# Two attention blocks in fp32 on one core: layer 1's value product as a two-level product, its row sums on VectorE and its differences on GpSimd, with other ends

## The chip, the cores and the metric

The kernel runs on one core of a Trainium2 chip. A time is the time in microseconds of one execution of the whole program on the device. Three executions of the kernel before took 2806.8, 2808.33 and 2808.77 us; their median, 2808.33 us, stands for it. A further execution was taken with the hardware profiler: that is where all shorter times in this text come from. TensorE is called PE in the profile, VectorE DVE, ScalarE ACT, GpSimd POOL, and SyncE, which issues nearly all the transfers, SP.

## The reference

The input is a batch of 8 images with 512 channels and 32 x 32 = 1024 positions. Two attention blocks follow one another, each with its own weights. In short:

```python
def block0(x):                                # 32 groups, 8 heads of 64 channels
    h = group_norm(x, gn_weight, gn_bias)     # per image and group
    q, k, v = split_by_head(w_qkv @ h + b_qkv)
    weight = softmax((q * scale)^T @ (k * scale))   # 1024 x 1024 per head
    a = weight @ v
    return x + w_proj @ a + b_proj

def block1(x):                                # 8 groups, one head of 512 channels
    h = group_norm(x, gamma, beta)
    q, k, v = (conv1x1(h, w, b) for w, b in ((q_w, q_b), (k_w, k_b), (v_w, v_b)))
    o = softmax((q^T @ k) * 512 ** -0.5) @ v
    return x + conv1x1(o, p_w, p_b)

out = block1(block0(x))
```

All of it is in float32.

## The kernel before

**Products in halves.** Every product of two large matrices is done by the Strassen-Winograd scheme: both factors are cut in two by two, seven products of quarters take the place of eight, and sums of quarters are formed before and after. `wino` (L229) does this on one level: products 1, the four of `middle`, 4 and 3, in this order, the last two put off into the list `tail`, so that the next product's first matmuls come between. `conv2` (L508) does it on two levels, 49 products in all, with the steps of `inner_steps` (L439). There, results are added up in SBUF by VectorE (`add`, L526, and L537 in the groups) and by GpSimd (`more`, L539 and L542). The sums of an image's quarters that two levels need, the dictionary `inner`, are formed once by `inner_factors` (L410) on GpSimd; those of a weight are formed in the prologue (`prepare`, `keep` and `keep2`), stored in DRAM (`wdram` one level, `wdram2` two), and loaded for each use by `load_weight` in the order of the list `uses`, through three buffers. A two-level weight takes two loads (1792 and 1344 KB), a one-level weight one (1792 KB).

**Layer 1's matrices are folded.** Queries and keys become one matrix m, so the scores are h^T m h, with g = m h; the value and the output convolution become one matrix z. Per image layer 1 has four products: g (`layer1_scores`, two levels), the scores (`scores1`, one level outside and one inside), z (L1093, `by_token`, one level: 56 matmuls of 256 columns) and the weighted sum (`values1`, one level). In layer 0 the convolutions v, k, q and p are two-level products, and the attention goes head by head.

**The order.** The loop over b interleaves the layers: layer 0's attention of image b, then layer 1 of image b-1 (g, scores, z, weighted sum), then v, k and q of image b+1 and the projection of image b. The first image's v, q and k, and the weights' preparation, are in `prologue`, and the first attention (b = 0) still carries a part of that preparation, in the lists `later` that name the attention step at which each is issued. Image 7 goes without partner, so the last layer 1 stands alone at the end. Each engine works off its own queue in program order. Where an operation of VectorE or GpSimd isn't tied to a place by `keep_in_program_order`, a scheduler sets it among its neighbours. Small work is handed over as lists: `hooks` (run after a product), and `background`, from which `run_background` takes a few after each product.

**Around the change.** In `scores1` seven outer products s = 0..6 stand for p = 1, 2, 5, 6, 7, 3, 4. In each, PSUM tiles are added into the eight tiles `e` by VectorE (L729), and in s = 3 and s = 4 also among themselves by GpSimd (`more`, L734). `exps` (L737) turns a quarter into exponentials on ScalarE once it is complete. `add_up` (L741) then adds the eight quarters' halves into `total`, the rows' sums over the keys (up to the partition sum, which TensorE does in `sums`): on GpSimd, L743. Last, `right_sums` (L163, used at L786) forms four differences of exponentials, t1, t2, t4 and b22 - b12, for the weighted sum: the two 128x1024 tiles of the first two on VectorE and of the last two on GpSimd. In `values1`, `done` (L797) turns a finished quarter of the output into x + (product * 1/sum) + bias with three VectorE operations (L802, L803, L805) and stores it.

Of the kernel before, what the change touches and what calls it, by code (L numbers as in the profile page):

```python
# [29 lines left out]
def two_attention_blocks_kernel(  # L30
# [143 lines left out]
    def main_path(ctx):  # L174
# [54 lines left out]
        def wino(uid, mm, done, middle=(6, 2, 5, 7), hooks=(), after=(), back=2):  # L229
# [12 lines left out]
            def step(p):  # L242
                n = bank[p]
                for i in range(2):
# [11 lines left out]
                    elif p == 7:  # L256
                        upper(u3, i, "w")
                        done(i, 1, 1, ps["c", i], u3[i])
                    elif p == 4:
                        done(i, 1, 0, ps["b", i], t1[i])  # L260
                    elif p == 3:
                        done(i, 0, 1, ps["c", i], u2[i])
# [31 lines left out]
        def keep(n, t):  # L294
            nc.sync.dma_start(wdram[n], t)


        wdram2 = {n: dram.tile([P, 7, 7, P], F32, name=f"sums2_{n}") for n in "qkmvp"}

        def keep2(n, t, engine=nc.gpsimd):  # L300
# [9 lines left out]
            for dst, x, y, op in (  # L310
                (s1, a21, a22, ALU.add), (s2, s1, a11, ALU.subtract), (s3, a11, a21, ALU.subtract),
                (s4, a12, s2, ALU.subtract),
            ):
                tc.keep_in_program_order(engine.tensor_tensor(dst, x, y, op))
            for j, f in enumerate((a11, a12, s4, a22, s1, s2, s3)):
                nc.sync.dma_start(wdram2[n][:, :, j, :], f)
# [4 lines left out]
        for b in range(1, B - 1):  # L321
            uses += [*twice["m"], "z", *layer0, *twice["p"]]
        uses += ["p", *twice["m"], "z"]
        uses += [*twice["m"], "z"]
# [385 lines left out]
        def scores1(f, gf, gsteps, first, uid, stats):  # L710
# [8 lines left out]
            parts = [pair_tile(f"sum{r}_{uid}") for r in range(2)]  # L719
# [21 lines left out]
            def add_up(r, c):  # L741

                on = lambda dst, x, y: lambda: tc.keep_in_program_order(nc.gpsimd.tensor_tensor(dst, x, y, ALU.add))  # L743
                if r == c:
                    return [on(parts[r], e[c, 0, r], e[c, 1, r])]
                return [
                    *(on(parts[r], parts[r], e[c, cc, r]) for cc in range(2)),
                    on(total[:, r, :], parts[r][:, 0, :], parts[r][:, 1, :]),
                ]

            def product(s, p, y, x, before, small, after7=(), final=()):
# [21 lines left out]
            product(3, 6, (1, 0), (1, 0), [7, 3], [])  # L773
            product(4, 7, (1, 0), (1, 0), [], stats[5:7])
            product(5, 3, (0, 1), (0, 1), [], stats[7:10] + add_up(0, 0), [lambda: exps(1, 1)], [lambda: exps(0, 1)])
            product(
                6, 4, (1, 0), (1, 0), [], stats[10:] + add_up(1, 1) + add_up(0, 1), (),
                [lambda: exps(1, 0), lambda: background.extend(add_up(1, 0) + steps)],
            )

            t = [[pair_tile(f"t{n}_{uid}_{cc}") for cc in range(2)] for n in (1, 2, 4)]
            engines = [nc.vector] * 4 + [nc.gpsimd] * 4
            fs, steps = right_sums(
                [(e[0, cc, 0], e[0, cc, 1]) for cc in range(2)], [(e[1, cc, 0], e[1, cc, 1]) for cc in range(2)],
                [lambda cc, n=n: t[n][cc] for n in range(3)],
                lambda *a: engines.pop(0).tensor_tensor(*a, ALU.subtract),  # L786
            )
            return total, {p: [x[:, i, :] for x in fs[p] for i in range(2)] for p in fs}

        def values1(b, zf, ef, r, xt, uid, hooks):  # L790
            def mm(p, i, ps, start):
                for k in range(4):
                    matmul(
                        ps, zf[p][k // 2][:, k % 2, ts(i, P)], ef[p][k], start=start and k == 0, stop=k == 3, skip_group_check=True
                    )
# [607 lines left out]
```

## Time and profile before

| | us |
|---|---|
| median of three executions | 2808.33 |
| the profiled execution | 2808.09 |
| its span, from the first to the last instruction | 2806.3 |
| TensorE busy | 2786.6 |
| VectorE busy | 1981.4 |
| GpSimd busy | 1265.5 |
| ScalarE busy | 986.3 |
| the first attention (119.38 to 242.33) | 122.95 |
| the second attention (331.70 to 447.56) | 115.86 |
| TensorE's clock, granted share over the span | 0.998 |

Busy time is the time in which an instruction of the engine ran; the span less the busy time is idle. Matmuls overlap one another, so the duration of one matmul in the list of groups is longer than its share of the time; the distance from one start to the next is its cost. A line of a group gives the line of the code, the engine, the operation, output and inputs with the shapes, how many there were, their busy time and mean duration in ns, and the idle time ahead of them with the instruction that ended it. A line of the timeline gives start and duration in us first, for several instructions of one kind in a row (x2) as one. An fp32 matmul leaves two records in the trace.

### The profile page before, as it was taken

Reading aid. Unit: us, or ns where it says so; the run is one execution under the profiler, and the core shown is the slowest. Engines: PE = TensorE matmul, PEld = TensorE weight load, DVE = VectorE, ACT = ScalarE, POOL = GpSimd, SP = SyncE. Lnnn points to the kernel's source line nnn. Section 1 sums busy time; section 2 is a strip of 40 time slices with the busy share of each in tenths; the row PEclk is TensorE's granted clock in tenths of the full one; section 3 lists DMA queues with packets and bytes.
Section 4 is the critical chain, followed back from the end, with each engine's and each line's share of the span. In section 5 each row is a group of like instructions: output and inputs, shape, how many; then the busy total and the mean of one; then the engine's idle time right before and its main releaser. Section 6 shows DMA issues by size and latency. Waiting matters only on the chain.

```text
span 2806.3 us, 35081 instructions
## 1 busy us (share of the span) xinstructions
PE 2786.6 (99%) x12756; PEld 1749.4 (62%) x12756; DVE 1981.4 (71%) x3018; ACT 986.3 (35%) x1275; POOL 1265.5 (45%) x1300
## 2 busy tenths in 40 slices
PE   9999999999999999999999999999999999999999
PEld 5436736776376853768538594485844868348584
DVE  5477777667776777766776767766678756787665
ACT  1253354214632146312463125531255212633130
POOL 2302705745067440774308652185521846137572
PEclk9999999999999999999999999999999999999999
DMA  8744512234123441134401343114521035112301
GB/s 285 226 161 139 196 32 70 111 146 178 34 67 131 152 153 39 62 139 165 148 24 62 150 174 127 32 54 161 187 102 49 37 151 207 63 55 94 120 5 73
DMA packets 118525, 320.10 MB, mean 114 GB/s; under 512 B 19591, under 2 KB 57927, under 8 KB 107722
## 3 DMA queue, kind: packets, MB, share of 16 engines
q1 hardware_dynamic: 117758, 317.36, 31.7%
q8 instruction: 103, 1.69, 0.2%
q14 instruction: 76, 0.62, 0.1%
q10 hardware_dynamic: 588, 0.42, 0.0%
HBM read 247.13 MB, written 70.62 MB: 113 GB/s over the span
## 4 chain that ended last, share of the span: by engine, by line
PE 97%; DVE 2%; issue 1%; POOL 1%; DMA 0%; ACT 0%; SPq 0%; DVEq 0%; POOLq 0%
PE sc L60 16%; PE av L60 15%; PE psb_av L60 6%; PE psb L60 5%; PE psa_av L60 4%; PE psc_av L60 4%; PE psc L60 3%; PE psa L60 3%; PE psb_z L60 3%; PE psb_g L60 3%; PE psb_k L60 3%; PE psb_q L60 3%; PE psb_v L60 3%; PE psb_p L60 2%; PE psa_z L60 2%; PE psc_z L60 2%
## 5 line engine op out<-in xcount | busy, mean ns | idle before, releaser
L658 ACT ACTIVATE e<-sc 128x1024 f32<-128x1024 f32 x512 | 476.2, 1051 | 79.7 <-PE sc L60 79.7
L662 DVE TENSOR_TENSOR sum<-sum,e 128x1024 f32<-128x1024 f32 x384 | 470.5, 1225 | 35.8 <-ACT x L138 0.5
L60 PE MATMUL sc<-q,k 64*128 64x512 f32 x2048 | 458.4, 597 | 0.0
L60 PE MATMUL av<-e,v 128*64 128x512 f32 x2048 | 453.4, 595 | 0.0
L60 PEld LDWEIGHTS sc<-q,k 64*128 64x128 f32 x2048 | 190.7, 186 | 247.3 <-ACT e L658 120.3
L60 PEld LDWEIGHTS av<-e,v 128*64 128x64 f32 x2048 | 141.4, 137 | 299.0 <-issue 289.0
L421 POOL TENSOR_TENSOR inner_h<-x 128x256 f32<-128x256 f32 x16 | 14.8, 924 | 415.8 <-DVE x L1105 415.8
L660 DVE TENSOR_TENSOR sum<-e,e 128x1024 f32<-128x1024 f32 x64 | 79.2, 1237 | 103.7 <-ACT e L658 103.7
L681 ACT COPY a<-av 128x512 f32<-128x512 f32 x64 | 37.6, 587 | 319.4 <-PE av L60 308.1
L126 POOL TENSOR_TENSOR rstd<-ve,mhalf 128x4 f32<-128x4 f32 x16 | 16.7, 1043 | 263.9 <-DVE ve L124 263.9
L60 PE MATMUL psb<-inner,inner_h 128*128 128x256 f32 x448 | 115.6, 380 | 0.0
L60 PE MATMUL psa_av<-e,z 128*128 128x512 f32 x256 | 113.3, 595 | 0.0
L421 POOL TENSOR_TENSOR inner_h<-h 128x256 f32<-128x256 f32 x30 | 24.1, 805 | 186.9 <-DVE h L1105 119.8
L743 POOL TENSOR_TENSOR sum<-sum,e 128x1024 f32<-128x1024 f32 x32 | 81.4, 2543 | 28.9 <-ACT e L739 27.7
L60 PEld LDWEIGHTS psb<-inner,inner_h 128*128 128x128 f32 x448 | 84.5, 190 | 13.6 <-POOL inner L436 1.8
L469 ACT COPY psb_v<-psa_v 128x512 f32<-128x512 f32 (+1 forms) x28 | 14.5, 517 | 218.9 <-DVE x L805 155.1
L60 PE MATMUL psb_g<-inner_h,w_m 128*128 128x256 f32 x336 | 86.5, 385 | 0.3
L729 DVE TENSOR_TENSOR e<-psc,u 128x512 f32<-128x512 f32 x56 | 38.7, 691 | 65.5 <-PE psc L60 65.3
L542 POOL TENSOR_TENSOR v<-v,v 128x256 f32<-128x256 f32 x28 | 20.1, 727 | 143.5 <-DVE u_v L537 143.4
L60 PEld LDWEIGHTS psa_av<-e,z 128*128 128x128 f32 x256 | 48.0, 190 | 57.3 <-issue 56.6
L421 POOL TENSOR_TENSOR inner_h<-t_h 128x256 f32<-128x256 f32 x62 | 73.3, 1187 | 21.3 <-PE psc_av L60 16.1
L739 ACT ACTIVATE e<-e 128x1024 f32<-128x1024 f32 x64 | 65.3, 1053 | 46.7 <-DVE e L729 25.6
(433 smaller groups left out, 6088.6 us busy)
## 6 DMA issues: line engine op xcount, KB each, us to landing
r<-all_rows SPq DMA_DIRECT2D x78, 256.0 KB
x<-in_x SPq DMA_DIRECT2D x36, 512.0 KB
h<-in_x SPq DMA_DIRECT2D x32, 512.0 KB
spill<-x SPq DMA_DIRECT2D x32, 512.0 KB
x<-spill SPq DMA_DIRECT2D x32, 512.0 KB
out<-x SPq DMA_DIRECT2D x64, 256.0 KB
kept<-a SPq DMA_DIRECT2D x28, 512.0 KB
again<-kept SPq DMA_DIRECT2D x28, 512.0 KB
```

Source lines behind the costliest of these rows:

```text
L60: tc.keep_in_program_order(nc.tensor.matmul(*args, **kw))
L126: nc.gpsimd.tensor_tensor(rstd, ve, mhalf, ALU.pow)
L421: pin(engine.tensor_tensor(dst, x, y, ALU.subtract))
L469: nc.scalar.copy(ps["b"], ps["a"])
L542: nc.gpsimd.tensor_tensor(d, x, y, ALU.add)
L658: nc.scalar.activation(e, sc, AF.Exp, scale=(C // 8) ** -0.5)
L660: nc.vector.tensor_add(total, es[0], e)
L662: nc.vector.tensor_add(total, total, e)
L681: nc.scalar.copy(dst, av)
L729: nc.vector.tensor_add(dst[0], ps, x[0])
L739: nc.scalar.activation(e[c, cc, r], e[c, cc, r], AF.Exp, scale=scale)
L743: on = lambda dst, x, y: lambda: tc.keep_in_program_order(nc.gpsimd.tensor_tensor(dst, x, y, ALU.add))
```

## The change

Layer 1's z becomes a two-level product: `layer1_rest` calls `conv2` by tokens with the image's `inner`, which is kept until then. Its weight is prepared twice over in the first attention (`keep2_steps`, four GpSimd operations of 128x896 and seven stores of 448 KB each), and loaded in two parts per image. The result's layout is another, so `mm` in `values1` and `halves` index it differently.

In `scores1` the row sums move from GpSimd (six additions of 128x1024 and two of 128x512 per image) to VectorE: fourteen additions of 128x512 per image straight into `total`; three are handed over in product s = 3, three in s = 6, and eight after it, so that they fall into z's first products. The tiles `parts` are gone. The differences are now eight GpSimd operations in the order b12' = b22 - b12 (two), t2 = b12' + b11, t1 = b22 - t2, t4 = b21 - t2; the first two are handed over after z's second pair of products, the other six after its fourth.

In the last image `early` adds bias and x to the half-finished quarter ahead of the last product, and that product is cut in two column halves for its last tile, so that one multiplication, one addition and one store of half a tile remain per half. In the prologue `normed` is called one matmul earlier, and the preparation of k moves behind v. In the first attention z's preparation steps move from step 1 to step 3, and weight loads from steps 2, 2, 5 to steps 4, 12, 12. The layer 1 of image 6 gets the last image's group mean and affine steps two products earlier.

```diff
@@ -226,7 +226,7 @@
-        def wino(uid, mm, done, middle=(6, 2, 5, 7), hooks=(), after=(), back=2):
+        def wino(uid, mm, done, middle=(6, 2, 5, 7), hooks=(), after=(), back=2, early=None):
@@ -257,6 +257,8 @@
                     elif p == 4:
+                        if early:
+                            early(i, u2[i])
                         done(i, 1, 0, ps["b", i], t1[i])
@@ -292,12 +294,12 @@
         def keep(n, t):
-            nc.sync.dma_start(wdram[n], t)
-
-
-        wdram2 = {n: dram.tile([P, 7, 7, P], F32, name=f"sums2_{n}") for n in "qkmvp"}
-
-        def keep2(n, t, engine=nc.gpsimd):
+            return nc.sync.dma_start(wdram[n], t)
+
+
+        wdram2 = {n: dram.tile([P, 7, 7, P], F32, name=f"sums2_{n}") for n in "qkmvpz"}
+
+        def keep2_steps(n, t, engine=nc.gpsimd):
@@ -307,21 +309,32 @@
             s1, s2, s3, s4 = u
-            for dst, x, y, op in (
-                (s1, a21, a22, ALU.add), (s2, s1, a11, ALU.subtract), (s3, a11, a21, ALU.subtract),
-                (s4, a12, s2, ALU.subtract),
-            ):
-                tc.keep_in_program_order(engine.tensor_tensor(dst, x, y, op))
-            for j, f in enumerate((a11, a12, s4, a22, s1, s2, s3)):
-                nc.sync.dma_start(wdram2[n][:, :, j, :], f)
+            def store():
+                for j, f in enumerate((a11, a12, s4, a22, s1, s2, s3)):
+                    tc.keep_in_program_order(nc.sync.dma_start(wdram2[n][:, :, j, :], f))
+
+            return [
+                *(
+                    lambda dst=dst, x=x, y=y, op=op: tc.keep_in_program_order(engine.tensor_tensor(dst, x, y, op))
+                    for dst, x, y, op in (
+                        (s1, a21, a22, ALU.add), (s2, s1, a11, ALU.subtract), (s3, a11, a21, ALU.subtract),
+                        (s4, a12, s2, ALU.subtract),
+                    )
+                ),
+                store,
+            ]
+
+        def keep2(n, t, engine=nc.gpsimd):
+            for f in keep2_steps(n, t, engine):
+                f()
         twice = {n: [(n, 0), (n, 1)] for n in wdram2}
         layer0 = [*twice["v"], *twice["k"], *twice["q"]]
         uses = [*layer0, *twice["p"]]
         for b in range(1, B - 1):
-            uses += [*twice["m"], "z", *layer0, *twice["p"]]
-        uses += ["p", *twice["m"], "z"]
-        uses += [*twice["m"], "z"]
+            uses += [*twice["m"], *twice["z"], *layer0, *twice["p"]]
+        uses += ["p", *twice["m"], *twice["z"]]
+        uses += [*twice["m"], *twice["z"]]
         loaded = []
@@ -716,7 +729,6 @@
             total = pair_tile(f"sum_{uid}")
-            parts = [pair_tile(f"sum{r}_{uid}") for r in range(2)]
             g2 = {1: first}
@@ -740,13 +752,11 @@
-                on = lambda dst, x, y: lambda: tc.keep_in_program_order(nc.gpsimd.tensor_tensor(dst, x, y, ALU.add))
+                on = lambda *a: lambda: tc.keep_in_program_order(nc.vector.tensor_add(*a))
+                dst, terms = total[:, r, :], [e[c, cc, r][:, i, :] for cc in range(2) for i in range(2)]
                 if r == c:
-                    return [on(parts[r], e[c, 0, r], e[c, 1, r])]
-                return [
-                    *(on(parts[r], parts[r], e[c, cc, r]) for cc in range(2)),
-                    on(total[:, r, :], parts[r][:, 0, :], parts[r][:, 1, :]),
-                ]
+                    return [on(dst, *terms[:2]), *(on(dst, dst, t) for t in terms[2:])]
+                return [on(dst, dst, t) for t in terms]
@@ -770,42 +780,69 @@
             product(2, 5, (1, 1), None, [6, 4], gsteps[4:] + stats[3:5])
-            product(3, 6, (1, 0), (1, 0), [7, 3], [])
+            product(3, 6, (1, 0), (1, 0), [7, 3], add_up(0, 0))
             product(4, 7, (1, 0), (1, 0), [], stats[5:7])
-            product(5, 3, (0, 1), (0, 1), [], stats[7:10] + add_up(0, 0), [lambda: exps(1, 1)], [lambda: exps(0, 1)])
+            product(5, 3, (0, 1), (0, 1), [], stats[7:10], [lambda: exps(1, 1)], [lambda: exps(0, 1)])
             product(
-                6, 4, (1, 0), (1, 0), [], stats[10:] + add_up(1, 1) + add_up(0, 1), (),
-                [lambda: exps(1, 0), lambda: background.extend(add_up(1, 0) + steps)],
+                6, 4, (1, 0), (1, 0), [], stats[10:] + add_up(1, 1), (),
+                [lambda: exps(1, 0), lambda: background.extend(add_up(0, 1) + add_up(1, 0))],
             )
-            t = [[pair_tile(f"t{n}_{uid}_{cc}") for cc in range(2)] for n in (1, 2, 4)]
-            engines = [nc.vector] * 4 + [nc.gpsimd] * 4
-            fs, steps = right_sums(
-                [(e[0, cc, 0], e[0, cc, 1]) for cc in range(2)], [(e[1, cc, 0], e[1, cc, 1]) for cc in range(2)],
-                [lambda cc, n=n: t[n][cc] for n in range(3)],
-                lambda *a: engines.pop(0).tensor_tensor(*a, ALU.subtract),
-            )
-            return total, {p: [x[:, i, :] for x in fs[p] for i in range(2)] for p in fs}
+            t1, t2, t4 = ([pair_tile(f"t{n}_{uid}_{cc}") for cc in range(2)] for n in (1, 2, 4))
+            b11, b12, b21, b22 = ([e[c, cc, r] for cc in range(2)] for c in range(2) for r in range(2))
+            on = lambda *a: lambda: tc.keep_in_program_order(nc.gpsimd.tensor_tensor(*a))
+            steps = [
+                on(dst[cc], x[cc], y[cc], op) for dst, x, y, op in (
+                    (b12, b22, b12, ALU.subtract), (t2, b12, b11, ALU.add), (t1, b22, t2, ALU.subtract),
+                    (t4, b21, t2, ALU.subtract),
+                ) for cc in range(2)
+            ]
+            fs = {1: b11, 2: b21, 3: b22, 4: t4, 5: t1, 6: t2, 7: b12}
+            return total, {p: [x[:, i, :] for x in fs[p] for i in range(2)] for p in fs}, steps
+
         def values1(b, zf, ef, r, xt, uid, hooks):
+            last = b == B - 1
+
             def mm(p, i, ps, start):
-                for k in range(4):
-                    matmul(
-                        ps, zf[p][k // 2][:, k % 2, ts(i, P)], ef[p][k], start=start and k == 0, stop=k == 3, skip_group_check=True
-                    )
+                cut = 2 if last and (p, i) == (3, 1) else 1
+                for part in range(cut):
+                    cols = ts(part, HT // cut)
+                    for k in range(4):
+                        matmul(
+                            ps[:, cols], zf[p][i][:, ts(k, P)], ef[p][k][:, cols],
+                            start=start and k == 0, stop=k == 3, skip_group_check=True,
+                        )
+
+            def added(xh, o, oc):
+                nc.vector.scalar_tensor_tensor(xh, o, obias[1][:, oc : oc + 1], xh, ALU.add, ALU.add)
+
+            def early(i, u):
+                xh = xt[i][:, ts(1, HT)]
+                nc.vector.tensor_mul(u, u, r[:, 1, :])
+                added(xh, u, i)
             def done(i, row, c, ps, u):
                 oc = 2 * row + i
+                xh = xt[oc][:, ts(c, HT)]
+                dst = out[b, oc * P : (oc + 1) * P, ts(c, HT)]
+                if last and (row, c) == (0, 1):
+                    cut = 2 if i == 1 else 1
+                    for part in range(cut):
+                        cols = ts(part, HT // cut)
+                        nc.vector.tensor_mul(ps[:, cols], ps[:, cols], r[:, c, cols])
+                        nc.vector.tensor_add(xh[:, cols], ps[:, cols], xh[:, cols])
+                        nc.sync.dma_start(dst[:, cols], xh[:, cols])
+                    return
                 o = acc_tile(f"o_{uid}_{oc}_{c}") if (row, c) == (1, 1) else ps
                 if u is not None:
                     nc.vector.tensor_add(o, ps, u)
                 nc.vector.tensor_mul(o, o, r[:, c, :])
-                xh = xt[oc][:, ts(c, HT)]
-                nc.vector.scalar_tensor_tensor(xh, o, obias[1][:, oc : oc + 1], xh, ALU.add, ALU.add)
-                nc.sync.dma_start(out[b, oc * P : (oc + 1) * P, ts(c, HT)], xh)
-
-            wino(f"av_{uid}", mm, done, middle=(2, 5, 6, 7), hooks=hooks, back=4)
+                added(xh, o, oc)
+                nc.sync.dma_start(dst, xh)
+
+            wino(f"av_{uid}", mm, done, middle=(2, 5, 6, 7), hooks=hooks, back=4, early=early if last else None)
@@ -888,19 +925,19 @@
             product(
-                wq, wk, "m", {6: lambda: norm.group_mean(acc_tile("gmean_0_0")[:, :KC]), 9: normed},
+                wq, wk, "m", {6: lambda: norm.group_mean(acc_tile("gmean_0_0")[:, :KC]), 8: normed},
             )
             raw_v = raw("v", 6)
             raw_p = raw("p", 7)
             for f in first["v"][1]:
                 f()
             background.extend(steps)
-            for n in "qk":
-                background.extend(first[n][1])
+            background.extend(first["q"][1])
             v = by_token(weight_factors(first["v"][0]), hf, "v0_0", middle=(2, 5, 6, 7), back=4)
             finish()
             run_background(len(background))
             keep2("v", first["v"][0], nc.vector)
+            background.extend(first["k"][1])
             x1 = [load_x(1, c, "x1") for c in range(KC)] if B > 1 else []
@@ -924,9 +961,10 @@
             load = lambda: load_weight(tc.keep_in_program_order)
+            second = keep2_steps("z", t)
             later = {
-                1: steps, 2: [lambda: keep("z", t), load, load], 5: [load],
-                12: [
+                3: steps, 4: [load], 5: second[:1], 7: second[1:2], 9: second[2:3], 11: second[3:4], 12: [
+                    second[4], load, load,
                     lambda: tc.keep_in_program_order(nc.vector.tensor_copy(ubias, bias[0])),
@@ -1082,23 +1120,23 @@
             first = query_factors(gf[1], f"1_1_{b}")
-            total, ef = scores1(inner, gf, gsteps, first, f"1_{b}", stats)
+            total, ef, esteps = scores1(inner, gf, gsteps, first, f"1_{b}", stats)
             state = {}
             def sums():
                 state["r"] = reciprocals([total], f"1_{b}", True, nc.sync)
-            z = by_token(
-                weight("z"), hf, f"z1_{b}", hooks=[*hooks, [sums]], back=3,
-                after=[load_weight, lambda: background.extend(zsteps)],
+            z = conv2(
+                "z", inner, None, f"z1_{b}", [hooks[0], [*hooks[1], *esteps[:2]], [*hooks[2], sums], [*hooks[3], *esteps[2:]]],
+                after=[lambda: background.extend(zsteps)], by_tokens=True,
             )
             all_background()
             xt = [load_again(b, c, "x") for c in range(KC)]
-            stiles = [big_tile(f"sz{i}_{b}", (P, 2, 2, C // 2)) for i in (1, 2, 4)]
-            halves = lambda t: (t[:, :, : C // 2], t[:, :, C // 2 :])
+            stiles = [pair_tile(f"sz{i}_{b}") for i in (1, 2, 4)]
+            halves = lambda i, h: (z[i][:, ts(h, HT)], z[2 + i][:, ts(h, HT)])
             zf, zsteps = left_sums(
-                [halves(t) for t in z[:2]], [halves(t) for t in z[2:]],
-                [lambda j, t=t: t[:, j, :, :] for t in stiles], nc.vector.tensor_add, nc.vector.tensor_sub,
+                [halves(i, 0) for i in range(2)], [halves(i, 1) for i in range(2)],
+                [lambda j, t=t: t[:, j, :] for t in stiles], nc.vector.tensor_add, nc.vector.tensor_sub,
             )
@@ -1149,7 +1187,7 @@
                 ahead = [loads, *([f] for f in applies)]
-                layer1_rest(b - 1, inner, gf, gsteps, stats, [[], mean, [], affine], ahead)
+                layer1_rest(b - 1, inner, gf, gsteps, stats, [mean, affine, [], []], ahead)
                 break
             kept = apool.tile([KC, P, T], F32, tag="kept", name=f"kept_{b}")
```

## The prediction

> **What bounds the kernel now.** I read the page first: busy times, then the chain, then the groups by form, the waits of PE, and last the timeline where two engines meet.
>
> ```profile
> span 2806.3 us, 35081 instructions
> PE 2786.6 (99%) x12756; PEld 1749.4 (62%) x12756; DVE 1981.4 (71%) x3018; ACT 986.3 (35%) x1275; POOL 1265.5 (45%) x1300
> ...
> PE 97%; DVE 2%; issue 1%; POOL 1%; DMA 0%; ACT 0%; SPq 0%; DVEq 0%; POOLq 0%
> ```
>
> TensorE is never out of work except about 20 us. So there are three ways to a shorter time: fewer TensorE microseconds, the few waits, and the two ends. The list of PE's waits (us in total, times, longest) holds nearly all of the second:
>
> ```profile
> PE sums L60 <- DVE sum L662: 5.1, 1, 5.1
> ...
> PE psa_v L60 <- POOL h L140: 0.8, 1, 0.8
> PE psb_v L60 <- DVE w_v L240: 0.5, 1, 0.5
> ```
>
> Each came once: none recurs with the images. A stall that does recur would count eight times. The price of a matmul is its start-to-start distance, not the mean duration in the groups, since matmuls overlap. The timelines of PE in the value product of layer 0 (two-level) and in layer 1's z (one-level) show it:
>
> ```profile
> 589.72 1.06 PE L60 MATMUL psb_v<-w_v,inner_h 128*128 128x128 f32 x8
> 590.62 0.61 PE L60 MATMUL psa_v<-w_v,h 128*128 128x128 f32 x4
> ...
> 520.05 3.62 PE L60 MATMUL psa_z<-w_z,x 128*128 128x256 f32 x16
> 523.51 2.75 PE L60 MATMUL psc_z<-w_z,t_h 128*128 128x256 f32 x12
> ```
>
> Eight records of 128 columns go from 589.72 to 590.62: 0.112 us each. Sixteen of 256 columns go from 520.05 to 523.51: 0.216 each. An fp32 matmul leaves two records.
>
> The last view is of VectorE and GpSimd at the same time:
>
> ```profile
> 520.93 4.60 DVE L786 TENSOR_TENSOR t<-e,e 128x1024 f32<-128x1024 f32 x2
> 525.46 5.58 DVE L786 TENSOR_TENSOR t<-e,t 128x1024 f32<-128x1024 f32 x2
> ...
> 524.53 2.13 POOL L743 TENSOR_TENSOR sum<-sum 128x512 f32<-128x512 f32 x1
> 526.62 6.63 POOL L786 TENSOR_TENSOR e<-e,e 128x1024 f32<-128x1024 f32 x2
> ```
>
> The same VectorE form (L662) takes 1.225 alone, here 2.3 to 2.8; GpSimd's 2.35 becomes 3.3: they take turns. And in the scores, under L436 of GpSimd, a sum of 128x512 of two SBUF inputs takes 1.2 where it takes 0.68 alone, while the sum from PSUM beside it stays at 0.69:
>
> ```profile
> 485.75 1.17 POOL L436 TENSOR_TENSOR inner<-g 128x256 f32<-128x256 f32 x1
> 486.26 1.21 DVE L1079 TENSOR_TENSOR sg<-g,sg 128x512 f32<-128x512 f32 x1
> 487.52 0.69 DVE L729 TENSOR_TENSOR e<-psb,c 128x512 f32<-128x512 f32 x1
> ```
>
> **What the Trainium skill says.** "SBUF — State Buffer", section "Who interferes with whom": a VectorE instruction with two SBUF inputs and a GpSimd instruction that reads SBUF exclude each other for the whole instruction, and order decides who waits; one SBUF input does not contend. The lines above agree, number for number. "TensorE: Matmul & The Clock Gate", "Wait — 56ns, not 53.3ns?": a pass takes N/2.4 + 2.5 ns; two passes give 112 ns at 128 columns (trace 112) and 218 at 256 (trace 216). The same page, "What's actually happening": an idle window of about 3.4 us halves the clock; the trace has idle from 147.97 to 153.20 and a clock of 0.50 from 150.55 to 157.38. "GPSIMD Engine Reference", "4.1 Engine selection": two-input elementwise is about twice as slow on GpSimd; here 2.35 against 1.225.
>
> **The change part by part.** Base: profiled execution 2808.09 (span 2806.3 and 1.8 around it), 0.24 under the median of 2808.33.
>
> *z in halves twice.* Removed: 56 matmuls of 256 columns, 112 records x 0.2158 = 24.17 us per image. Added: 98 of 128 columns, 196 x 0.112 = 21.95. Gain 2.22 per image, 17.8 in eight.
>
> *New TensorE waits per image.* The order of work in the changed kernel can be followed engine by engine, and four places are late.
> (a) Product s=3 of the scores gets three row sums on VectorE, each between two PSUM sums that TensorE needs. A product is 7 steps of 0.863; six sums at a pitch of 0.61 fit, nine don't fit locally: u, sum, e, sum, c, sum, e. Uncontended the three push c to 3.1 and the next e to 4.3 us after the first starts; TensorE wants them at 3.2 and 4.05, so 0.4 is lost. But GpSimd runs L436 without pause to 494.1, through this stretch. At 1.16 each c is at 4.1 and e at 5.8: 1.85 lost. GpSimd's operations resume as each sum ends, so the second and third meet the tail of one (0.73 against 0.61 between sums); I take 0.8, ends 0.4 and 1.85.
> (b) Product s=6 has three more, GpSimd idle: 0.4 (0 to 0.6).
> (c) The last two exponentials (1.05 each) now stand on ScalarE ahead of z's first u copy (0.57). They start about 2.8 us into z, so the copy ends at 5.4; TensorE wants it at 5.3 less the release: 0.2 (0 to 0.4).
> (d) z's first two pairs: eight row sums lie among the pair sums in VectorE's order, and the first difference b12 - b22 on GpSimd (128x1024, 2.35) is released by the sixth of them. In us from z's start: the first pair's sum begins at 6.7, when its matmul is done; the sums run to 9.9 (sixth) and 10.6 (seventh). GpSimd then holds the port to 13.0. The second pair's two u sums read PSUM and pass, but the eighth row sum stands next in VectorE's queue and waits to 13.0, ends 13.7; behind it four pair sums (pitch 0.34, last 0.42) end at 15.0, and TensorE's step wants the last of them at 13.1. Loss 2.0. If GpSimd is first in the race behind the sixth sum, both last row sums are late and it is 2.9; if VectorE gets through, 0.3.
> The sum is 0.8+0.4+0.2+2.0 = 3.4, against the gain of 2.22: +1.2 per image, +9.4 in eight.
>
> *What lies beside other work.* GpSimd's six 128x1024 row sums (81.4 + 37.5 + 26.3 us in all) go away; it gets four more differences (4 x 2.35) and eight additions per image at 0.73, as v has: it stays below half busy. The t4 and t1 differences are done 5 us or more before product p=5 wants them; were they late, each us counts. The held `inner` factors cost loads of the next image some 10 to 15 us, with about 8 us or more in hand. The second z load (1344 KB) and the issues on SP stand behind transfers that have tens of us. I cost these at nothing; if a weight came late TensorE would wait us for us, which is in rival 3.
>
> *First attention.* prepare_z's four VectorE steps wait for a DMA until 141.38 (VectorE idle for 9.67), and the six sums behind them end at 153.12, which is PE's 5.1. Two hooks later the data is there and nothing queues behind it. Gain: 122.95 us for the first attention against 115.86 for the second, 7.1, which is 5.2 of idle and the half clock after it. Against it: four GpSimd operations (2.1 each, as L314) can each hold a VectorE sum up; seven stores of 512-byte pieces and two loads go to SP at hook 12, with v's next weights behind them. Value 7.1, ends 3 and 7.1.
>
> *Prologue.* The hook one matmul earlier (4 records x 0.216): 0.86; prepare_k's steps (40.68 to 43.29) out of the way of w_v: 0.7. Ends 0 and 1.6.
>
> *Last image.* After the last matmuls VectorE has 0.70 + 0.70 + 0.75, from 2799.39 to 2801.61:
>
> ```profile
> 2799.39 0.70 DVE L802 TENSOR_TENSOR psc_av<-psc_av,u_av 128x512 f32<-128x512 f32 x1 [1.21 <-PE psc_av L60]
> ...
> 2800.12 0.70 DVE L803 TENSOR_TENSOR psc_av<-psc_av,r 128x512 f32<-128x512 f32 x1
> 2800.86 0.75 DVE L805 SCALAR_TENSOR_TENSOR x<-psc_av,obias,x 128x512 f32<-128x512 f32 x1
> ```
>
> Then two operations of 256 columns at 0.42: 1.3 less, and a store of half the bytes, 0.3 to 0.7 less by estimate: 1.8.
>
> Sum: 2808.09 + 9.4 - 7.1 - 1.6 - 1.8 = 2807.0.
>
> **Rivals.**
> 1. *TensorE's gain is kept.* VectorE's row sums slip between, (d) costs 0.3 and (a) 0.4: waits of 1.3, -0.9 per image, -7.4, -10.5 at the ends: 2790; with no wait at all 2780. For it: VectorE is 71% busy, and v, which has this form, loses only 0.27. Against: v has no row sums among its pair sums.
> 2. *Slower: the shared port.* Every row sum of s=3 meets an L436 operation, and GpSimd wins the race in z: 1.85 + 0.4 + 0.2 + 2.9 = 5.4, +3.2 per image, +25 - 10.5: 2823; with one of the two at its middle value about 2816. It decides once the waits pass 2.22 + 10.5/8 = 3.5 per image. For it: the 1.21 above. Against: alternation hides part of each wait.
> 3. *The ends give little.* The idle in the first attention turns into another wait, of VectorE on GpSimd's four operations or of layer 0's v on its weights: 4 to 7 lost, 2811 to 2814.
>
> **How the numbers follow.** Forecast 0.36 (own range 2801 to 2812), rival 1 0.30, rival 2 0.20, rival 3 0.14. A difference under 0.2% (5.6 us) is about what a measurement of this kernel can't tell from none. The forecast's case gives faster 0.10, same 0.26; rival 1 faster 0.30; rival 2 same 0.02, slower 0.18; rival 3 faster 0.01, same 0.07, slower 0.06. Together 0.41, 0.35, 0.24. The range, 2786 to 2820, cuts the extremes of rivals 1 and 2.
>
> **What would show it.** In the changed profile: records of z at 0.112 and 21.95 per image; PE waits that recur eight times, psc_z on VectorE's c (2 us), the scores' psc and psb on VectorE (0.8 and 0.4), psb_z on ScalarE (0.2); no "sums <- sum" wait of 5.1; GpSimd's difference and VectorE's row sum alternating in z. The prediction is wrong if PE doesn't wait in z's second pair, if the row sums of s=3 take 0.68, or if the first attention stays above 118 us.

## The result and the profile after

The changed kernel takes 2815.12 us (median of nine executions, 2813.8 to 2817.66) against 2807.9 (median of nine, 2806.8 to 2809.11): 1.0026 times the time before, 95% interval 1.0016 to 1.0035. It is slower by 7.2 us, clear of the executions' spread. The page of its profiled execution begins:

```profile
span 2814.0 us, 36894 instructions
...
PE 2781.1 (99%) x13436; PEld 1758.4 (62%) x13436; DVE 2039.6 (72%) x3262; ACT 1000.7 (36%) x1307; POOL 1249.9 (44%) x1336
```

TensorE's busy time fell by 5.5 us, the span rose by 7.7. Busy time hides a part of a wait, since a matmul's record reaches over the start of the next; the starts show more. Cut at the first attention's start, at the start of image 1's v and at the last weighted sum (where it goes on behind z's last two products, at 2757.99 and 2766.05), the 7.7 us come from these stretches (profiled executions, us):

| stretch | before | after | difference |
|---|---|---|---|
| prologue, to the first attention | 119.3 | 125.8 | +6.5 |
| first attention | 122.95 | 115.69 | -7.3 |
| from image 1's v to the last weighted sum | 2515.7 | 2524.6 | +8.8 |
| last weighted sum to the end | 48.3 | 47.95 | -0.4 |

Here are the waits of TensorE in the changed kernel (in total, times, longest); the first attention's `sums` line of 5.1 is gone, and waits that come six to eight times are new. The two lines `tr_wv` and `psb_q` belong to the prologue:

```profile
PE psc_z L60 <- DVE c_z L550: 9.6, 7, 1.4
...
PE psc L60 <- DVE c L741: 3.4, 8, 0.5
PE tr_wv L63 <- DVE k L410: 3.3, 4, 2.1
PE psc_av L60 <- DVE sz L157: 2.3, 6, 0.4
PE psb_q L60 <- DVE w_q L240: 1.3, 1, 1.3
```

**One image.** The period of a steady image went from 341.89 us (673.72 to 1015.61) to 343.40 (1017.89 to 1361.29 in the changed kernel): +1.51, from the start of one image's attention to the next. The matmuls of z do what they should; the timeline of PE has sixteen records from 863.40 to 865.19, 0.112 us each:

```profile
863.40 1.95 PE L60 MATMUL psb_z<-w_z,inner_h 128*128 128x128 f32 x16
...
867.87 0.61 PE L60 MATMUL psa_z<-w_z,x 128*128 128x128 f32 x4
869.85 0.71 PE L60 MATMUL psc_z<-w_z,x 128*128 128x128 f32 x4 [1.37 <-DVE c_z L550]
```

The last line is the new wait: 1.53 us beyond the usual distance of the starts. VectorE's timeline at that time, and GpSimd's after it:

```profile
864.29 1.41 DVE L755 TENSOR_TENSOR sum<-sum,e 128x512 f32<-128x512 f32 x2
865.62 0.75 DVE L550 TENSOR_TENSOR u_z<-psb_z,z 128x256 f32<-128x256 f32 x2
866.28 2.18 DVE L755 TENSOR_TENSOR sum<-sum,e 128x512 f32<-128x512 f32 x1
868.39 0.74 DVE L550 TENSOR_TENSOR z<-psa_z,z 128x256 f32<-128x256 f32 x2
869.05 0.74 DVE L550 TENSOR_TENSOR c_z<-psc_z,z 128x256 f32<-128x256 f32 x2
```

```profile
865.15 2.77 POOL L793 TENSOR_TENSOR e<-e,e 128x1024 f32<-128x1024 f32 x1 [16.84 <-ACT z L472]
```

GpSimd's difference is issued when the sixth row sum ends (864.98), waits 0.4 us behind the seventh, runs to 867.92, and the eighth row sum takes 2.18 us where it takes 0.68 alone: as the prediction had it, a VectorE sum of two SBUF inputs and an operation of GpSimd shut each other out. What they share is called the port here. Four pair sums stand behind it. The two u sums that read PSUM (865.62) passed at once. In brackets the profile names a copy on ScalarE that ended at about the same time, 865.07; that the sixth row sum is what the difference waits for is read from the order of events, and run 5 below bears it out.

All differences of starts over the layer 1 of this image (image 1), with the restart of the matmul stream after each wait: 0.95 us in product s=3, 0.38 in s=6, 1.63 for c_z, 0.17 later in z, 0.63 in the weighted sum, together 3.76; less z's 2.22 this is 1.5. Image 6 is the exception, and an experiment that the kernel makes by itself: there GpSimd first waits for the last image's group statistics, so the difference starts at 2610.99, after the eighth row sum, and TensorE loses 0.25 us there instead of 1.53.

**The ends.** The waits on w_q and k fall into the prologue. VectorE's timeline there (start, duration):

```profile
98.55 0.69 DVE L291 TENSOR_TENSOR prepare_m<-prepare_m 128x512 f32<-128x512 f32 x1 [4.61 <-DMA prepare_m<-product_m]
99.16 0.75 DVE L410 SCALAR_TENSOR_TENSOR k<-psb_k,par,t_k 128x512 f32<-128x512 f32 x1
```

The result k stood ready in PSUM, but the sum for m ahead of it on VectorE waited for m's loads. In the kernel before the same sum ran earlier:

```profile
93.75 0.68 DVE L289 TENSOR_TENSOR prepare_m<-prepare_m 128x512 f32<-128x512 f32 x1
```

In the changed kernel TensorE was nearly idle from 99.3 to 103.1, and its clock was 0.50 from about 102.7 to 109.6. At the end of the program VectorE starts on the first half of the cut tile only when the matmuls of both halves are done (the last one starts at 2807.05):

```profile
2807.47 0.43 DVE L833 TENSOR_TENSOR psc_av<-psc_av,r 128x256 f32<-128x256 f32 x1 [2.03 <-PE psc_av L60]
...
2808.40 0.43 DVE L833 TENSOR_TENSOR psc_av<-psc_av,r 128x256 f32<-128x256 f32 x1
```

### The profile page after: what moved, and what is told of

Its sections match the earlier page's. It is cut to its first block, busy times and chain, and to the rows that moved or that the text cites. A ratio compares the mean times of both kernels' runs of the same rounds, so it can differ in the third digit from the quotient of the medians.

```text
span 2814.0 us, 36894 instructions
## 1 busy us (share of the span) xinstructions
PE 2781.1 (99%) x13436; PEld 1758.4 (62%) x13436; DVE 2039.6 (72%) x3262; ACT 1000.7 (36%) x1307; POOL 1249.9 (44%) x1336
## 5 line engine op out<-in xcount | busy, mean ns | idle before, releaser
L793 POOL TENSOR_TENSOR e<-e,e 128x1024 f32<-128x1024 f32 x16 | 40.5, 2536 | 122.3 <-ACT z L472 117.9
L60 PE MATMUL psb_z<-w_z,inner_h 128*128 128x128 f32 x672 | 87.9, 277 | 0.3 <-DVE u_z L550 0.3
L60 PEld LDWEIGHTS psb_z<-w_z,inner_h 128*128 128x128 f32 x672 | 81.7, 192 | 1.6 <-DVE u_z L550 0.5
L482 ACT COPY psb<-psa 128x512 f32<-128x512 f32 x56 | 31.9, 570 | 137.1 <-PE psa L60 137.1
```

What stands on the lines that cost most here:

```text
L60: tc.keep_in_program_order(nc.tensor.matmul(*args, **kw))
L482: nc.scalar.copy(ps["b"], ps["a"])
L793: on = lambda *a: lambda: tc.keep_in_program_order(nc.gpsimd.tensor_tensor(*a))
```

## The experiments

The theory behind the first runs has two causes, apart from one another. In every image but one GpSimd's first difference shuts out a row sum (D); in the prologue the pinned order of stores on SP makes m's loads late (P). Medians are given, most with that of the kernel before in the same comparison. The cuts of code show the lines that matter; where a run needs more, the text says so.

**1. The prologue's stores unpinned.**

```diff
-    tc.keep_in_program_order(nc.sync.dma_start(wdram2[n][:, :, j, :], f))
+    pin(nc.sync.dma_start(wdram2[n][:, :, j, :], f))
```

Here `pin` does nothing where `keep2` calls, and keeps the order for z.

> The changed kernel, with the prologue's stores of the two-level weights (v, q, k, m, p) free of their pinned order on SP; z's stores keep theirs. Theory P (the pinned stores hold up m's loads, these m's four VectorE sums, and these the last results of k): the waits of TensorE on k at about 100 us and the half clock after them go, some 5 to 6 us, so about 2809 against 2815.1. Rival K (k's four preparation steps, moved into q's convolution, do it): 2815, the waits stay.

2807.74 us, ratio to before 0.9999 (0.9991 to 1.0007): 7.4 less than the changed kernel. SP's timeline of the changed kernel and then of this one:

```profile
87.17 5.32 SPq L314 DMA_DIRECT2D sums_k<-prepare_k  x5
92.53 2.69 SPq L286 DMA_DIRECT2D prepare_m<-product_m  x2
```

```profile
81.68 2.41 SPq L314 DMA_DIRECT2D sums_k<-prepare_k  x3
84.21 3.76 SPq L286 DMA_DIRECT2D prepare_m<-product_m  x4
```

With pins, five stores of k, which wait for GpSimd's preparation, stand ahead of two of m's four loads; without, the loads go out from 84.21. The wait on k falls to 0.5 us, the one on w_q is gone, and so is the half clock. P holds. The rival falls: k's steps were still in q's convolution.

**2. The kernel before, with these stores pinned.**

```diff
-    nc.sync.dma_start(wdram2[n][:, :, j, :], f)
+    tc.keep_in_program_order(nc.sync.dma_start(wdram2[n][:, :, j, :], f))
```

> The kernel before, with only the order of the prologue's two-level stores on SP pinned. Theory P: TensorE waits on k at about 100 us for 3 to 4 us and runs at half clock after it; 2812 to 2814 against 2807.9, less what the first attention's idle gives back. Rival K: 2808, no such wait.

2813.55 against 2808.26, ratio 1.0018 (1.0011 to 1.0026). The pin alone costs 5.3 us, with the same waits (3.4 on k, 1.2 on w_q); the first attention's wait falls from 5.1 to 3.8, so a part is given back. The half clock behind these waits lasts 3.4 us here and 6.8 in the changed kernel, which is a part of the difference between 5.3 and 7.4. P holds from this side too.

**3. Both b22 - b12 differences a pair later.**

```diff
-    [hooks[0], [*hooks[1], *esteps[:2]], [*hooks[2], sums], [*hooks[3], *esteps[2:]]],
+    [hooks[0], hooks[1], [*hooks[2], sums, *esteps[:2]], [*hooks[3], *esteps[2:]]],
```

> The changed kernel, with the first two GpSimd differences (b22 - b12) handed over after z's third pair of products instead of the second. Theory D (GpSimd's difference shuts VectorE's eighth row sum out, and the pair sums behind it): TensorE's wait on c_z falls from 1.53 to about 0.25 us, as image 6 has it, in seven images: 9 us less, 2806. Rival F (VectorE has too much in these two pairs, whoever holds the port): the wait stays above 1 us, 2814 to 2815.

2852.09 us, 1.0156 (1.0143 to 1.017): neither. The wait on c_z is gone, as D says, but a larger one has come, in TensorE's waits:

```profile
PE psb_av L60 <- DVE u_av L240: 32.3, 6, 5.4
```

In GpSimd's order the two differences now came behind five of z's own sums (at 879.96 in image 1), and all that follows was late: its last differences, the scaling of layer 0 and the next image's sums held the port to 908 while VectorE made the sums of z. TensorE then idled 5.4 us, and its clock was 0.50 after it. I had taken GpSimd to have room here.

**4. The kernel before, with only the first attention's order changed.**

```diff
-    1: steps, 2: [lambda: keep("z", t), load, load], 5: [load],
+    3: steps, 4: [lambda: keep("z", t), load, load], 5: [load],
```

> The kernel before, with only the first attention's order changed: z's preparation sums at step 3 instead of step 1, and its store and the first two weight loads at step 4. Theory A (the 5.1 us wait and the half clock are all of the excess, and nothing comes in their place): 7.1 us less, 2800.8. Rival W (another wait, of v or k on its weights, takes its place): 2803 to 2808.

2802.44 against 2808.26, ratio 0.9979 (0.9971 to 0.9987): 5.8 less, between A and W but near A. The wait `sums` is 1.7 instead of 5.1, so a rest of it stays in this kernel, where z's sums and loads move by two steps; the half clock is gone. In the changed kernel, which moves them otherwise, the wait is gone altogether.

**5. The two differences exchanged.** The first is then released by the last row sum.

```diff
-    [*hooks[1], *esteps[:2]]
+    [*hooks[1], *esteps[1::-1]]
```

> The changed kernel, with the first two GpSimd differences exchanged: the first one issued is now released by VectorE's last row sum, not by its sixth, so no row sum can meet it; GpSimd's work is otherwise where it was, about 1 us later. Theory D (the port shut by this one difference): TensorE's wait on c_z falls from 1.53 to about 0.25 us in seven images, 9 us less, 2806, and none of the 5.4 us waits of the kernel that issued both differences a pair later. Rival L (any later difference makes the last sums of z late in the weighted sum): the wait is exchanged for another, 2812 or more.

2805.63, 9.5 less than the changed kernel, ratio to before 0.9992 (0.9983 to 1.0). VectorE's eighth row sum, and GpSimd's differences behind it:

```profile
865.97 0.68 DVE L755 TENSOR_TENSOR sum<-sum,e 128x512 f32<-128x512 f32 x1
866.83 4.68 POOL L793 TENSOR_TENSOR e<-e,e 128x1024 f32<-128x1024 f32 x2 [18.83 <-DVE sum L755]
```

No wait of z on c_z is left in the list. D holds: the price of the port in this place was 9.5 us over the program, and VectorE does have room for all eight row sums in z's first pairs. L doesn't come: the wait on `sz` grows from 2.3 to 3.1 us in all.

**6. Both.**

> The changed kernel with both: the exchange, and the prologue's stores unpinned. If the two causes are apart, their gains add: 2815.1 - 7.4 - 9 = 2798.7. If they overlap or the exchange fails: 2803 to 2808.

2800.43 against 2807.92, 0.9972 (0.9961 to 0.9982). The gains of 7.4 and 9.5 would add up to 2798.2; the executions of this kernel lie between 2797.0 and 2801.7, so they add within that spread. The profiled execution, 2797.02, is the fastest of them. TensorE's remaining waits that recur:

```profile
PE psc_av L60 <- DVE sz L157: 3.1, 6, 0.5
PE psc L60 <- DVE c L741: 3.0, 7, 0.5
```

Image 1's v starts at 233.4, 8.8 us earlier than before, near the 7.1 + 0.86 + 0.7 that the prediction had for the first attention and the prologue. (1.6 of it is the prologue; in the seven other profiled executions with unpinned stores the prologue gains 0.9 to 1.8.)

**7. With both, the first three row sums in product s=5.**

```diff
-    product(3, 6, (1, 0), (1, 0), [7, 3], add_up(0, 0))
-    product(5, 3, (0, 1), (0, 1), [], stats[7:10], [lambda: exps(1, 1)], [lambda: exps(0, 1)])
+    product(3, 6, (1, 0), (1, 0), [7, 3], [])
+    product(5, 3, (0, 1), (0, 1), [], stats[7:10] + add_up(0, 0), [lambda: exps(1, 1)], [lambda: exps(0, 1)])
```

> As the kernel with both, and the first three row sums handed over in product s=5 instead of s=3, where GpSimd has nothing to do. Theory P (of the 0.77 us lost in s=3 the larger part is GpSimd's): 0.25 to 0.4 us lost in s=5 in its place, 3 to 4 us less than the kernel with both. Rival V (VectorE's three extra sums cost the same anywhere): no difference.

2799.92, 0.9976 (0.9966 to 0.9986): no difference from 6 beyond the spread of the executions. TensorE loses 0.86 + 0.17 us in s=5 where it lost 0.62 + 0.17 in s=3. That looks like Rival V, but both sides of the expectation took GpSimd to be idle in s=5, and the trace of this run shows that it wasn't when the first row sum came (image 0):

```profile
493.73 2.50 POOL L746 TENSOR_TENSOR e<-e,e 128x512 f32<-128x512 f32 x2 [0.29 <-DVE e L741]
495.29 1.49 DVE L755 TENSOR_TENSOR sum<-e 128x512 f32<-128x512 f32 x1
```

The row sum takes 1.49 us for 0.68 and ends 0.55 us after GpSimd's addition (496.23). So the run moved the row sums from one GpSimd operation to another, and doesn't decide between P and V. Run 6 does, by chance. In s=3 its first row sum and an operation of GpSimd start within 0.02 us of each other. In image 1 GpSimd is first, in image 2 VectorE:

```profile
824.83 0.72 POOL L449 TENSOR_TENSOR inner<-sg 128x256 f32<-128x256 f32 x1
824.85 1.26 DVE L755 TENSOR_TENSOR sum<-e 128x512 f32<-128x512 f32 x1
...
1166.87 1.28 POOL L449 TENSOR_TENSOR inner<-sg 128x256 f32<-128x256 f32 x1
1166.88 0.68 DVE L755 TENSOR_TENSOR sum<-e 128x512 f32<-128x512 f32 x1
```

The second and third sums take 0.68 in both. Up to the first matmul of s=4, product s=3 takes 6.91 us in image 1 and 6.33 in image 2, against 6.04 in the kernel before; with the 0.11 that s=4 loses in either case, 0.98 and 0.40 are lost. So three row sums in one product cost 0.4 us by themselves, as in s=6 with GpSimd idle (0.38), and the port adds 0.58 where GpSimd is first. The changed kernel's first row sum in s=3 takes 1.24 to 1.25 us in images 0 to 5, so there the port adds about as much. P holds as to the cause; s=5 was no place without GpSimd.

**8. With both, the last tile not cut.**

```diff
-    cut = 2 if last and (p, i) == (3, 1) else 1
+    cut = 1
```

> As the kernel with both, and the last image's last tile not cut in column halves (one multiplication, one addition, one store). If the cut lets VectorE start on the first half early, the end grows by about 0.4 us or more. If both halves wait for the tile's last matmul anyway, as the trace of the changed kernel shows, the end from the last matmul to the last instruction doesn't grow, or shrinks by up to 0.4 us (1.4 us of VectorE instead of 1.8).

The cut of `done` (the second `cut = 2` of the diff) goes with it. From the start of the small matmul behind the last product to the end of the span: 7.01 us, against 6.39 with the cut in run 6 (and 6.63 in the changed kernel, 7.02 in the kernel before). Both halves do wait for the tile's last matmul, and VectorE needs 0.4 us less without the cut, yet the end is 0.6 later, so neither reading of the expectation fits. This run is a single execution. In all traces of this document the end takes 6.36 to 6.78 us with the cut (ten) and 7.00 to 7.06 without it (four), so the cut seems to shorten it, though three of the four differ in more than the cut; what it gives lies behind VectorE, with the stores, and why isn't settled.

**9. With both, the three row sums one each in s=3, 4 and 5.**

```diff
-    product(3, 6, (1, 0), (1, 0), [7, 3], add_up(0, 0))
-    product(4, 7, (1, 0), (1, 0), [], stats[5:7])
-    product(5, 3, (0, 1), (0, 1), [], stats[7:10], [lambda: exps(1, 1)], [lambda: exps(0, 1)])
+    product(3, 6, (1, 0), (1, 0), [7, 3], add_up(0, 0)[:1])
+    product(4, 7, (1, 0), (1, 0), [], stats[5:7] + add_up(0, 0)[1:2])
+    product(5, 3, (0, 1), (0, 1), [], stats[7:10] + add_up(0, 0)[2:], [lambda: exps(1, 1)], [lambda: exps(0, 1)])
```

> As the kernel with exchange and unpinned stores (2800.4), and the first three row sums handed over one each in products s=3, 4, 5 instead of three in s=3. Theory V (a product has room for one more VectorE sum, not for three between neighbours; GpSimd has little to do with it, since three in s=5 cost the same): the 0.8 us lost in s=3 go, nothing comes in s=4 and 5; about 6 us less, 2794. Rival P (each sum that meets GpSimd costs TensorE): 0.2 to 0.4 us lost in s=3 and in s=4 each, 2797 to 2800.

2796.66 against 2807.22, 0.9964 (0.9951 to 0.9978): the fastest version that computes the whole result. By the medians it is 3.8 us less than 6, but the executions of the two overlap (2796.5 to 2799.4 here), and by the traces the scores are only 0.2 us shorter per image. In s=3 0.08 us is lost and in s=4 0.16, but 0.54 in s=5, where V expected nothing. The single row sums meet GpSimd in all three: they take 1.26, 1.33 and 1.70 us (image 0), in s=5 because of L746 again. The loss grows with their length, so a product bears one row sum that the port delays by about 0.6 us, and not one delayed by 1.0. Neither V's account, which leaves GpSimd out, nor P's 0.2 to 0.4 each fits.

The profiled execution of this version is 11.5 us shorter than that of the kernel before. Of these, 7.3 lie in the first attention, 1.3 in the prologue, 2.1 after the start of image 7's v, and 0.8 in the six image periods between. So of the 2.22 us per image that the two-level z saves, 0.13 is left: the waits on VectorE in the scores (1.2), in z (0.4) and in the weighted sum (0.6) take the rest.

**10. Then t2 on VectorE.**

```diff
-    on(dst[cc], x[cc], y[cc], op) for dst, x, y, op in (
+    on(dst[cc], x[cc], y[cc], op, nc.vector if dst is t2 else nc.gpsimd) for dst, x, y, op in (
```

`on` takes the engine from this last argument.

> As the one with the sums spread, and the two differences t2 on VectorE, which is idle at the end of z, instead of GpSimd. Theory G (GpSimd's four more differences run into VectorE's sums of z at the start of the weighted sum and make them late, 0.67 us per image): GpSimd is through 2 us earlier or more and the wait of the weighted sum on sz goes, about 3 to 4 us less than with the sums spread. Rival H (it is the layer 0 scaling and the next image's sums behind the differences that hold the port): the wait stays above 0.4 us, no difference.

2806.71, 0.9999 (0.999 to 1.0007): 10 us more than 9. GpSimd waited for VectorE's t2 and was through at 882.3, no earlier than in 9 (881.9), and the sums of z came one place later in VectorE's order, behind the second output tile, so the wait on sz grew to 1.8 us and 12.0 in all. Neither G's gain nor H's "no difference" came, and the question stays open by this run.

**11. The scores' sums and differences as before, under the two-level z** (stores unpinned).

```diff
-    on = lambda *a: lambda: tc.keep_in_program_order(nc.vector.tensor_add(*a))
+    on = lambda dst, x, y: lambda: tc.keep_in_program_order(nc.gpsimd.tensor_tensor(dst, x, y, ALU.add))
```

The rest of the edit, not shown, brings back `parts`, `right_sums` with its four differences on VectorE, and the old places of both.

> The changed kernel with its stores unpinned and with the scores' row sums and differences as before (row sums and four differences on GpSimd, four on VectorE). Theory N (the two-level z needs GpSimd for its own sums while it would still be adding up rows and taking differences): z waits for GpSimd several us per image, 2830 or more. Rival R (GpSimd catches up; the row sums on VectorE were only a cost): 2.2 us less per image than before on TensorE, nothing in its place, 2785 to 2795.

2851.93 (two executions), 1.0159 (1.014 to 1.0177), with waits of up to 8.5 us of psb_z on u_z in all eight images, 50.9 in total. N holds by its number, and without the new scores the two-level z would cost far more than it saves. The way is another than N's: in image 1 the sum u_z stands on VectorE behind the four old differences, which lie among z's sums (858.38 to 868.37) and take 2.3 to 2.5 us each, since GpSimd's row sums and differences run at the same time. The run puts row sums and differences back together, so it doesn't say what each is worth.

**12. As 9, without the differences t4.**

> As the kernel with the first row sums spread, with the last two differences (t4) left out: the fourth product takes b21 in their place, so this part of the result isn't the layer's. GpSimd is through 4.7 us earlier. Theory G (the differences added on GpSimd push the scaling of layer 0 into VectorE's first sums of z): the weighted sum's wait on sz, 0.5 us in six images, goes; 3 to 4 us less than 2796.7. Rival H (the scaling and the next image's sums meet the sums of z wherever they stand): the wait stays above 0.4 us.

2792.12, 4.5 less than 9, and the wait on sz is gone from the list. G holds as to the cause, the differences added on GpSimd. The scaling of layer 0 in run 9 and here:

```profile
881.93 2.36 POOL L709 TENSOR_TENSOR a<-a,r 128x1024 f32<-128x1024 f32 x1
...
876.44 2.35 POOL L709 TENSOR_TENSOR a<-a,r 128x1024 f32<-128x1024 f32 x1
```

It is out of the way here: z's first sum comes at 880.84, in run 9 at 882.51. But one of the sums of z also stood a place earlier in VectorE's order, so that all of the 0.5 us comes from the port isn't shown.

## Why the prediction was wrong

The forecast was 2807.0, no change to speak of, with faster (0.41) held likelier than slower (0.24). The measured 2815.1 is slower beyond its noise, though within the wide range. The step that failed is the cost of nothing that the prediction gave to "the issues on SP": the prologue's stores, pinned in order, hold up m's loads and cost 7.4 us. The reading of what bounds the kernel held, and so did most steps:

- *z in halves twice*: 0.112 us per record, 2.22 per image, as predicted.
- *(d)*: the mechanism held to the order of events. VectorE won the race behind the sixth sum, the eighth row sum stood shut out (2.18 us), and four pair sums stood behind it. It measured 1.53 for 2.0. Run 5 shows the cause. Image 6, without it, wasn't foreseen.
- *(a)*: 0.8 predicted, 0.95 measured with the restart, and the two parts were right too: 0.4 for three sums in one product, and about as much again from GpSimd's L436 (L449 in the changed kernel), measured as 0.58 in run 6. But it is the first row sum that meets GpSimd, not the second and third: these take 0.68, which the prediction named as a sign of being wrong.
- *(b)*: 0.4, measured 0.38. *(c)*: 0.2, measured nothing.
- *What lies beside other work*, a smaller failure: the four more differences on GpSimd were costed at nothing, since TensorE wants them late. But they push what stands behind them on GpSimd into VectorE's sums of z: 0.63 us in six images (run 12, with the reserve made there). I asked who waits for the differences, not who waits behind them.
- *First attention*: 7.1, measured 7.3; nothing took its place. Rival 3 was right that the ends would give little, but not about where: it was the prologue.
- *Prologue*, the failure that decided it: 1.6 gained was near for the two edits that I priced (run 6; 0.9 to 1.8 elsewhere), but the diff also pins the order of the two-level stores in `keep2_steps`, which `keep2` calls for every weight of the prologue. I read the pin as part of z's new stores, and wrote that the issues on SP stand behind transfers that have tens of us. By the difference of run 1 and the changed kernel it costs 7.4 us, alone in the kernel before 5.3. The prologue lost 6.5 instead of gaining 1.6, 8.1 us, as much as the distance from 2807.0 to 2815.1; the other misses about cancel. Without the pin the kernel takes 2807.74 (run 1), next to the forecast.
- *Last image*: 1.8 predicted, 0.4 measured. My sum left only one half's two operations behind the last matmul; but both halves wait for the tile's last matmul, so four are left. Nor does a shorter VectorE time pass on to the end: in run 8 it has 0.8 us less to do there than in the kernel before, and the end takes as long (7.01 and 7.02, one execution each).

So +1.2 per image was +1.5 in the steady images, near enough, and the ends gave 1.2 us instead of 10.5. Rival 2's "about 2816" (its sums give 2814.2 and 2815.4) is close to the measured time by luck: it puts the whole loss on the images' waits, which were 3.76 us, nearer to the forecast's 3.4 than to the 4.3 or more of this rival.

## What to carry to other kernels

A wrapper that pins an order acts on every caller: follow each changed helper to all its callers, and on the queue that it issues to, ask what stands behind an entry that waits. When work is moved away from an engine to test whether that engine is the cause, see in the trace that it was idle in the new place: run 7 moved the row sums from one GpSimd operation to another, and its time alone would have cleared GpSimd. When work is moved to an engine, price what then stands behind it there, not only its own consumer. Where VectorE reads two SBUF operands near a GpSimd operation, let the GpSimd operation be released by the last of them rather than by an earlier one: here exchanging two instructions was worth 9.5 us, while handing both over a pair later cost 37. And a saving in TensorE's time is worth only what the waits beside it leave: here 0.13 of 2.22 us per image.

## What the runs showed that I had not expected

In the changed kernel TensorE's clock fell to 0.50 at about 102.7 though the idle time was broken up, with a transpose at 99.96 and one at 102.42 between waits of 0.67 and 2.13 us. "TensorE: Matmul & The Clock Gate", section "What's actually happening", gives an idle window of about 3.4 us. Here waits of 2.80 us in all, with single matmuls between them, were enough, and in the kernel before the clock fell at 150.55, 2.4 us after the last matmul had ended (148.12). So these traces don't fit a rule that asks for 3.4 us without any matmul. The half clock then lasted 6.83 us in both kernels, 3.41 in the prologue of run 2.
